# Two layers of attention on one core: a reciprocal, a normalisation and a fold change places in the queues

## The chip, the cores and the metric

One core of one Trainium2 chip runs the whole program. The time is device microseconds of that core, the median of several executions. Engines are named as in the profile: PE is TensorE (matmuls), DVE is VectorE, ACT is ScalarE, POOL is GpSimd, SP is SyncE. Each works through its own queue in order. POOL and SP are used here mostly to issue DMAs.

## The reference

Two layers of the same form, on x of 16 images x 256 channels x 32 x 32, all in float32:

```python
def _L0_conv_ref(x, Wq, bq, Wk, bk, Wv, bv, rel_h, rel_w):
    q = proj(Wq, bq); k = proj(Wk, bk); v = proj(Wv, bv)      # 4 heads of 64, n = 1024
    sim = jnp.einsum('bhdi,bhdj->bhij', q, k)
    rel = (rel_h + rel_w).reshape(heads, d, n)
    qpos = jnp.einsum('hdi,bhdj->bhij', rel, q)
    attn = jax.nn.softmax(sim + qpos, axis=-1)
    out = jnp.einsum('bhdn,bhmn->bhdm', v, attn)
x = x + _L0_conv_ref(_gn(x), ...)       # _gn: 16 groups over the last axis, mean and variance
x = x + _L1_conv_ref(_gn(x), ...)
```

## The kernel before

A **unit** is one image in one layer; there are 32, in an order that leaves several units between the two layers of one image. A unit has four **blocks**: two pairs of heads (`pr`), and for each pair two halves of 512 query columns. The program counts blocks through as n = 4u + b, and "first" to "fourth block" below means b = 0 to 3. All four have their own order, written out by hand: the function `block` serves the second and third block (b = 1, 2), `block_with_q` the first, `block_with_values` the fourth, and `block_without_pieces` the end of the last unit. An engine takes its instructions in just the order in which these functions issue them.

In a block, for each of eight tiles j of 128 keys: DVE writes the positional term as a **seed** into PSUM (`seed`, L442), PE adds the scores (`scores`, L478), ACT takes the exponential into a tile p (L487). Ten p tiles are in rotation. Then PE multiplies p with the values into po (`attend`, L532), and ACT copies po to `od` (`take_out`, L594). The result isn't divided by the softmax's sum until much later, since that sum takes a long way round:

- DVE adds up the p tiles into `acc` (`add_up`, L517 and L519). POOL adds the last one or two of them by accumulating DMAs (`add_last`, L550), each waiting for the one before.
- POOL folds the upper 64 partitions of acc onto the lower (`fold`, L555); SP copies the first 32 of the rest into rows of a `stack` (`stack_up`, L569, two DMAs), and POOL adds the other 32 to the same rows (`fold_again`, L574, two DMAs). Two blocks of one pair of heads share a stack.
- POOL folds the stack in five steps, 64 rows down to 4 (`fold_stack`, L579), spread over the blocks that follow; SP copies the four rows that remain into `den_all` (`spread_sums`, L587, four DMAs).
- DVE takes the reciprocals (`reciprocals`, L629), 16 values on each of 128 partitions. SP writes them to a DRAM tile `rd` (L631) and reads them back spread over all partitions as `rden` (L636, two DMAs).
- DVE multiplies `od` by `rden` (`normalise`, L644), POOL adds the result to x by DMA (`add_by_dma`, L662), and for the second layer SP stores x (`store`, L667).

This takes about a unit: the second block of a unit handles the sums of the first pair of heads of the unit before (`before = blocks[n - 5][:2]`), the fourth block those of its second pair. In both, `reciprocals(*before)` comes early in the block and `normalise(*before)` near its end.

Between these stand pieces of work for coming units: projections, values, and the group norm. In the fourth block the norm's variance for the unit after the next is completed: PE forms a mean, DVE reduces it (`var`, L235), POOL raises it to the power -1/2 (`rstd`, L237) and multiplies once more (`nshift`, L239). In the listing this is `mean_out()`, and in the second block `mean_out()` is the reduction to `neg` (L219), which uses DVE alone.

Before the change, the second block's stack copies and reciprocals stand like this in SP's and DVE's order (L812 to L826):

```python
        if previous and folded:
            stack_up(previous)
        ...
        add_up(blk, 2)
        if before:
            reciprocals(*before)
```

`stack_up(previous)` waits for the fold of the first block, which POOL issues in this same second block.

Of the kernel before, what the change touches and what calls it, by code (L numbers as in the profile page):

```python
# [52 lines left out]
def fast_path(ctx, tc, sh, x, layers, out, W, den_all, good, flag):  # L53
# [457 lines left out]
    def add_up(blk, j):  # L511
        u, pr, half = blk
        if j == 0:
            return
        if j == 1:
            accs[blk] = apool.tile([P, 2, HALF], F32, tag="acc", name=f"acc_{u}_{pr}_{half}")
            nc.vector.tensor_tensor(accs[blk], probs[blk, 0], probs[blk, 1], ALU.add)  # L517
        else:
            nc.vector.tensor_tensor(accs[blk], accs[blk], probs[blk, j], ALU.add)  # L519
# [149 lines left out]
    def finish(u, pr):  # L669
        normalise(u, pr)  # L670
        add_residual(u, pr)
# [85 lines left out]
    def block(n):  # L757
        blk = blocks[n]
        u, b = divmod(n, BPU)
        pr_, half = blk[1:]  # L760

        stacked = blocks[n - 3][:2] if half == 1 and n > 2 else None
        summed = blocks[n - 4][:2] if half == 0 and n > 3 else None
        last_unit = u + 1 == NU
        before = blocks[n - 5][:2] if b == 1 and n > 4 else None
        after = blocks[n + 1] if n + 1 < len(blocks) else None
        previous = blocks[n - 1] if n > 0 else None
        one, two = u + 1 < NU, u + 2 < NU

        pieces = u + 1 < NU or b < 2  # L770
        if u + 1 == NU and b == 1:
            widen(u, 1)
        f0, f1, f2, f3 = ring
        folded = n - 1 < FOLDED
        if not pieces:
            return block_without_pieces(n, half)
        if b == 0 and u > 0:
            return block_with_q(n)
        if b == 3:
            return block_with_values(n)  # L780

        if previous and folded and b == 1:
            add_last(previous, NT - 2)
        elif previous:
            add_up(previous, 6)
            if folded:
                add_last(previous)
            else:
                add_up(previous, 7)
        if b == 2:  # L790
            add_inputs(u + 1, 0)
        for j in range(1 if n > 0 else 2, 4):
            scores(blk, j)
        (first, first_out), (second, second_out) = prepare(u, b)
        first(0)
        norms(u, b, 0)
        if n == 1:
            reduced(2, 1)
            added(2)
        seed(blk, 4, f1)  # L800
        scores(blk, 4)
        add_up(blk, 1)
        norms(u, b, 1)
        second(0)
        if half == 1:
            second_out()
        if stacked:
            fold_stack(*stacked, D)
        if summed:
            fold_stack(*summed, R // 8)  # L810
            spread_sums(*summed)
        if previous and folded:  # L812
            fold(previous)
        if stacked:
            fold_stack(*stacked, R)
        first(1)
        first_out()
        seed(blk, 5, f0)
        scores(blk, 5)
        if previous and folded:  # L820
            stack_up(previous)
        if b == 2 and n > 5:
            store(*blocks[n - 6][:2])
        add_up(blk, 2)
        if before:
            reciprocals(*before)  # L826
        if b == 2:
            add_inputs(u + 1, 1)
        if n == 0:
            reduced(2, 0)  # L830
        if half == 0:
            second(1)
            second_out()
        seed(blk, 6, f1)
        scores(blk, 6)
        if half == 0:
            ring[2:] = f3, f2
        seed(blk, 7, ring[2])
        scores(blk, 7)
        add_up(blk, 3)  # L840
        if b == 2:
            add_inputs(u + 1, 2)
        add_up(blk, 4)

        if after:
            seed(after, 0, f0)
        if n in check:
            next(checks)
        norms(u, b, 2)
        po = psum2(ring[3], f"po_{n}")  # L850
        values_of_p = attend(blk, po)
        values_of_p(0)
        if two and half == 1:
            mean_out = norm_mean(u + 2, filled(f1, f"pm_{n}", 0.0))
        if after:
            scores(after, 0)
        if n == 0:
            mean_out = norm_var(1, filled(f1, f"pm_{n}", EPS / 2))
        if stacked:
            fold_stack(*stacked, R // 2)  # L860
        if previous and folded:
            fold_again(previous)
        if half == 1 and u + 3 < NU and units[u + 3][1] == 0 and u > 0 or n == 3:
            load_x(units[u + 3][0], range(pr_, pr_ + 1) if u > 0 else range(CC))
        add_up(blk, 5)
        if n in (2, 6):
            W.mix(n // 4)
        if before and last_unit:
            finish(*before)
        elif before:  # L870
            normalise(*before)
            add_by_dma(*before)
        if two and half == 1 or n == 0:
            mean_out()
        if stacked:
            fold_stack(*stacked, R // 4)
            if n == len(blocks) - 3:
                fold_stack(*stacked, R // 8)
                spread_sums(*stacked)
        if after:  # L880
            for j in range(1, 4):
                seed(after, j, ring[j % 3])
        norms(u, b, 3)
        values_of_p(1)
        take_out(blk, po)
        pos[n] = po
# [55 lines left out]
    def block_with_values(n):  # L942

        blk = blocks[n]
        u = blk[0]
        r0, r1, r2, r3 = ring
        previous, after, stacked = blocks[n - 1], blocks[n + 1], blocks[n - 3][:2]
        before = blocks[n - 5][:2] if n > 4 else None
        two = u + 2 < NU
        v = Values(u + 1, psum2(r3, f"pw_{u + 1}"))  # L950

        add_last(previous, NT - 2)
        scores(blk, 1)
        add_up(blk, 1)
        one = v.half(1, HI, False), v.half(1, LO, True)
        two_halves = score_half(blk, 2, 0), score_half(blk, 2, 1)
        v.stage("1", (two_halves[0], two_halves[1]), (one[0], one[1]), 0)
        scores(blk, 3)
        v.stage("1", (two_halves[0], two_halves[1]), (one[0], one[1]), 1)
        v.keep(0, 0, 1.0)  # L960
        exponential(blk, 2)
        ab, ab_out = positions(u + 1, 0, psum2(r1, f"pa_{u + 1}_0"))
        ab(0)
        ab_out()
        v.pair("2", 6, 2, 0)
        seed(blk, 4, r0)
        scores(blk, 4)
        v.pair("2", 6, 2, 1)
        v.keep(1, 0, 1.0)
        seed(blk, 5, r2)  # L970
        scores(blk, 5)
        if before:
            reciprocals(*before)
        seed(blk, 6, r1)
        scores(blk, 6)
        v.combine(0, 0, ALU.add)
        fold_stack(*stacked, D)
        fold(previous)
        v.pair("3", 5, 7, 0)
        seed(blk, 7, r0)  # L980
        scores(blk, 7)
        v.pair("3", 5, 7, 1)
        v.keep(1, 1, -1.0)
        fold_stack(*stacked, R)
        stack_up(previous)
        add_up(blk, 2)
        seed(after, 0, r1)
        v.combine(1, 1, ALU.subtract)
        add_up(blk, 3)
        if n in check:  # L990
            next(checks)
        po = psum2(r2, f"po_{n}")
        values_of_p = attend(blk, po)
        values_of_p(0, range(5))
        v.pair("4", 3, 4, 0)
        if two:
            for pr in range(CC):
                bias_x(u, pr)
            mean_out = norm_var(u + 2, filled(r0, f"pm_{n}", EPS / 2))
        values_of_p(0, range(5, NT))  # L1000
        scores(after, 0)
        v.pair("4", 3, 4, 1)
        v.keep(0, 1, -1.0)
        add_up(blk, 4)
        if two:
            mean_out()
        fold_stack(*stacked, R // 2)
        fold_again(previous)
        if u + 3 < NU and units[u + 3][1] == 0:
            load_x(units[u + 3][0], range(1, 2) if u > 0 else range(CC))  # L1010
        ring[:] = r1, r0, r3, r2
        seed(after, 1, r0)
        if before:
            normalise(*before)
        v.combine(1, 0, ALU.add)
        fold_stack(*stacked, R // 4)
        seed(after, 2, r3)
        if before:
            add_by_dma(*before)
        add_up(blk, 5)  # L1020
        seed(after, 3, r1)
        values_of_p(1)
        take_out(blk, po)
        pos[n] = po
# [192 lines left out]
    mean_out = norm_mean(1, pm1)  # L1217
# [322 lines left out]
```

## Time and profile before

| | |
|---|---|
| three runs | 3065.86, 3075.89, 3077.37 us, median 3075.89 |
| profiled execution | 3064.96 us |
| its span, first to last instruction | 3063.2 us |
| mean granted TensorE clock | 0.929 of full speed |
| PE busy | 2593.9 us (85%) |
| DVE busy | 2229.4 us (73%) |
| ACT busy | 2017.4 us (66%) |
| POOL busy | 969.8 us (32%) |
| DMA share of 16 engines | 39.6% issued by POOL, 10.1% by SP |

The span starts with the first instruction and ends with the last; what lies around it is 1.8 us. In each view a group is named by line, engine, operation and the tiles it writes and reads (`od<-od,rden` writes od from od and rden). "idle before <-X" is the time for which the engine stood still ahead of an instruction, and X is what released it. POOL's and SP's rows are the issuing of DMAs; the data land later. The page gives the median time from issue to landing of each kind: 5.1 us for `acc<-p`, 3.5 for `acc<-acc`, 2.1 for `stack<-acc` from SP, 3.1 for `stack<-acc` from POOL, 2.9 for `den_all<-stack`, 2.2 for `rd<-r`, 4.4 for `rden<-rd`, 4.9 for `x<-od`.

### The profile page before, as it was taken

To read this page: it belongs to the slowest core of one execution; us is meant where nothing else is said; L and a number is where in the kernel's file an instruction comes from. 1 tells how busy PE (TensorE), PEld (TensorE's weight loads), DVE (VectorE), ACT (ScalarE), POOL (GpSimd) and SP (SyncE) were. 2 spreads that over 40 slices of the span, in tenths; PEclk is the share of its full clock that TensorE was granted. 3 is DMA by queue.
4 is the path that set the end of the run, shared out by engine and by line. 5 is a ranking of instruction groups with operands and counts; after the bars stand their busy time and mean duration, and the time that the engine had idled before them with its cause. 6 is when DMAs were issued, how large, how long until landed. Compare 5 with 4: busy or idle time off the path is not lost. (4 is left out here: it accounts for less than half of the span.)

```text
span 3063.2 us, 94037 instructions
## 1 busy us (share of the span) xinstructions
PE 2593.9 (85%) x41192; PEld 1453.6 (47%) x41192; DVE 2229.4 (73%) x2184; ACT 2017.4 (66%) x3977; POOL 969.8 (32%) x1029
## 2 busy tenths in 40 slices
PE   8898888978889878898888988789887897878888
PEld 4554444544455444454445544355444554445444
DVE  8786676866768767686676866668766686667878
ACT  7776666766667666675666766667666675667644
POOL 1333233332333323333233332333323333233321
PEclk9999999999999989998999999899999998989999
DMA  3444454555455454555545555454555544544553
GB/s 96 94 88 91 94 98 92 101 112 109 97 105 109 91 100 98 105 95 96 112 95 105 95 98 103 89 117 92 102 115 104 97 83 95 102 88 89 102 106 86
DMA packets 141905, 302.32 MB, mean 99 GB/s; under 512 B 56360, under 2 KB 57896, under 8 KB 141488
## 3 DMA queue, kind: packets, MB, share of 16 engines
q0 software_dynamic: 75744, 210.33, 39.6%
q1 hardware_dynamic: 65744, 85.90, 10.1%
q8 instruction: 326, 5.34, 0.7%
q14 instruction: 91, 0.75, 0.1%
HBM read 51.78 MB, written 17.30 MB: 23 GB/s over the span
## 5 line engine op out<-in xcount | busy, mean ns | idle before, releaser
L487 ACT ACTIVATE p<-ps,shift 128x1024 f32<-128x1024 f32 x993 | 1072.9, 1113 | 845.6 <-PE ps L478 833.1
L478 PE MATMUL ps<-q,k 64*64 64x512 f32 x7944 | 1048.7, 628 | 429.0 <-DVE ps L442 420.9
L442 DVE TENSOR_TENSOR ps<-abt 128x1024 f32<-128x1024 f32 x1018 | 1227.1, 1227 | 190.7 <-ACT p L487 130.0
L532 PE MATMUL po<-p,v 64*64 64x256 f32 x16384 | 943.2, 377 | 15.1 <-ACT q L279 15.1
L532 PEld LDWEIGHTS po<-p,v 64*64 64x64 f32 x16384 | 655.8, 133 | 319.5 <-issue 48.3
L478 PEld LDWEIGHTS ps<-q,k 64*64 64x64 f32 x7944 | 316.0, 139 | 854.5 <-issue 658.9
L519 DVE TENSOR_TENSOR acc<-acc,p 128x1024 f32<-128x1024 f32 x550 | 670.9, 1220 | 2.8
L550 POOL DMA_DIRECT2D acc<-p x217 | 226.0, 1042 | 654.0 <-ACT p L487 168.2
L644 DVE TENSOR_TENSOR od<-od,rden 128x1024 f32<-128x1024 f32 x63 | 77.6, 1231 | 470.4 <-DMA rden<-rd 470.4
L579 POOL DMA_DIRECT2D stack<-stack x310 | 307.0, 990 | 135.9 <-DMA stack<-stack 117.8
L574 POOL DMA_DIRECT2D stack<-acc x248 | 222.0, 1054 | 391.4 <-DMA stack<-acc 384.4
L268 PE MATMUL pq<-xn,Wq 64*64 64x512 f32 x2048 | 246.3, 595 | 0.0
L268 PE MATMUL pk<-xn,Wk 64*64 64x512 f32 x2048 | 243.2, 589 | 0.0
L555 POOL DMA_DIRECT2D acc<-acc x124 | 102.1, 823 | 439.4 <-DMA acc<-p 433.9
L517 DVE TENSOR_TENSOR acc<-p,p 128x1024 f32<-128x1024 f32 x128 | 156.2, 1220 | 92.4 <-ACT p L487 92.4
L248 ACT ACTIVATE xn<-x,nshift,rstd 128x128 f32<-128x128 f32 x496 | 209.6, 494 | 0.0
L237 POOL TENSOR_TENSOR rstd<-var,mhalf 128x16 f32<-128x16 f32 x31 | 122.9, 3964 | 238.3 <-DVE var L235 238.3
L190 ACT ACTIVATE junk<-x,neg 128x128 f32<-128x128 f32 x505 | 198.3, 399 | 0.0
L594 ACT COPY od<-po 128x512 f32<-128x512 f32 x127 | 74.4, 586 | 136.6 <-PE po L532 136.6
L268 PEld LDWEIGHTS pq<-xn,Wq 64*64 64x64 f32 x2048 | 82.2, 138 | 151.2 <-issue 142.4
L190 ACT ACTIVATE junk<-x 128x128 f32<-128x128 f32 x464 | 140.2, 313 | 0.0
L363 PE MATMUL pw<-mixed,t 64*64 64x128 f32 x2976 | 135.6, 271 | 1.8 <-issue 1.8
(96 smaller groups left out, 1921.1 us busy)
## 6 DMA issues: line engine op xcount, KB each, us to landing
acc<-p POOLq DMA_DIRECT2D x217, 512.0 KB, 5.1
rden<-rd SPq DMA_DIRECT2D x126, 256.0 KB, 4.4
acc<-acc POOLq DMA_DIRECT2D x124, 256.0 KB, 3.5
x<-od POOLq DMA_DIRECT2D x61, 512.0 KB, 4.9
x<-in_x_dram SPq DMA_DIRECT2D x32, 512.0 KB, 5.3
stack<-acc SPq DMA_DIRECT2D x248, 64.0 KB, 2.1
stack<-acc POOLq DMA_DIRECT2D x248, 64.0 KB, 3.1
out_dram<-x SPq DMA_DIRECT2D x31, 512.0 KB, 2.9
```

Source lines behind the costliest of these rows:

```text
L190: nc.scalar.activation(junk, grouped(xt[units[u][0]], g), func, accum_out=into[:, g : g + 1], **bias)
L248: nc.scalar.activation(grouped(xns[u], g), grouped(xt[units[u][0]], g), AF.Identity, bias=shift[:, g : g + 1], scale=rstd[:, g : g + 1],)
L268: yield nc.tensor.matmul(pk[c, nh, :], w[l][rs, cc, c0 : c0 + D], xns[u][rs, cc, nh * HALF : (nh + 1) * HALF], start=(t == 0 and cc == 0), ...
L442: nc.vector.tensor_tensor(ps.rearrange("p h (w y) -> p h w y", y=H), ab[:, :, :H].unsqueeze(2).to_broadcast([P, 2, XH, H]), ab[:, :, H + h ...
L478: nc.tensor.matmul(ps[c, h, :], a[hs, j0 : j0 + D], b[hs, columns], start=bool(tag) and i == 0, stop=i == len(terms) - 1, skip_group_check ...
L487: nc.scalar.activation(p, ps, AF.Exp, bias=W.shift)
L517: nc.vector.tensor_tensor(accs[blk], probs[blk, 0], probs[blk, 1], ALU.add)
L519: nc.vector.tensor_tensor(accs[blk], accs[blk], probs[blk, j], ALU.add)
L532: yield nc.tensor.matmul(po[c, a, :QUART], vts[u][rs, pr, j, h * D : (h + 1) * D], p[rs, h, a * QUART : (a + 1) * QUART], start=(t == 0 an ...
L550: nc.gpsimd.dma_start(accs[blk], probs[blk, j], accum_op=ALU.add)
L574: nc.gpsimd.dma_start(at, acc[R:D, h, :], accum_op=ALU.add)
L579: nc.gpsimd.dma_start(stack[:rows_], stack[rows_ : 2 * rows_], accum_op=ALU.add)
```

## The change

Three moves, and no instruction is added or removed. In the second block `reciprocals` goes from behind the second sum to just behind the first sum: on DVE ahead of one seed and one sum, on SP ahead of the two stack copies. In the second block of all units but the last, `normalise` and `add_by_dma` go from ahead of `mean_out()` to behind the three seeds for the block that follows: on DVE behind the reduction to `neg` and three seeds, on POOL behind one fold of the stack. In the fourth block one `fold_stack` and `fold_again` go ahead of `mean_out()`, so on POOL ahead of the power; the sum and the load that are moved with them stay as they were in the queues of DVE and SP.

```diff
@@ def block (second and third block) @@
         scores(blk, 4)
         add_up(blk, 1)
+        if before:
+            reciprocals(*before)
         norms(u, b, 1)
...
         add_up(blk, 2)
-        if before:
-            reciprocals(*before)
         if b == 2:
...
         if before and last_unit:
             finish(*before)
-        elif before:
-            normalise(*before)
-            add_by_dma(*before)
         if two and half == 1 or n == 0:
             mean_out()
         if stacked:
...
             for j in range(1, 4):
                 seed(after, j, ring[j % 3])
+        if before and not last_unit:
+            normalise(*before)
+            add_by_dma(*before)
         norms(u, b, 3)
@@ def block_with_values (fourth block) @@
         v.keep(0, 1, -1.0)
-        add_up(blk, 4)
-        if two:
-            mean_out()
         fold_stack(*stacked, R // 2)
         fold_again(previous)
         if u + 3 < NU and units[u + 3][1] == 0:
             load_x(units[u + 3][0], range(1, 2) if u > 0 else range(CC))
+        add_up(blk, 4)
+        if two:
+            mean_out()
         ring[:] = r1, r0, r3, r2
```

## The prediction

> **What bounds the kernel now.** I read the waits first, then the windows, then the order of time on SyncE (SP), VectorE (DVE) and GpSimd (POOL) through one unit in the middle of the run.
>
> The waits, columns: who waited for whom, us in total, times, longest:
>
> ```profile
> DVE od L644 <- DMA rden<-rd: 470.4, 30, 18.0
> PE ps L478 <- DVE ps L442: 420.9, 34, 16.3
> ACT p L487 <- DMA acc<-p: 8.2, 4, 3.3
> ```
>
> Thirty times, once in each of the 30 units from the second to the last but one, the normalisation (L644) of a second block holds DVE for 470.4/30 = 15.7 us until the reciprocals have come back spread out as rden. The seeds stand behind it on DVE, so TensorE (PE) is starved: 420.9 us is 90% of its idle time, since 3063.2 - 2593.9 = 469.3 us. The windows (PE, PEld, DVE, ACT, POOL busy, then clock, DMA share, GB/s) show a saturated PE before and nothing during:
>
> ```profile
> 1560.00:1574.00 14.00, 14.00 (x244) 7.35 (x240) 11.59 (x12) 12.74 (x30) 4.08 (x5) 1.00 0.42 77
> 1574.00:1588.00 14.00, 2.08 (x40) 1.18 (x32) 0.00 (x0) 2.33 (x6) 4.30 (x6) 0.74 0.58 111
> 1588.00:1600.00 12.00, 9.13 (x72) 3.25 (x76) 11.84 (x12) 5.21 (x9) 3.86 (x5) 0.73 0.49 92
> ```
>
> Why rden is late is told by SP in order of time, columns start, length, instruction:
>
> ```profile
> 1556.73 2.89 SPq L587 DMA_DIRECT2D den_all<-stack  x4
> 1560.19 20.66 SPq L569 DMA_DIRECT2D stack<-acc  x4
> 1580.90 0.58 SPq L631 DMA_DIRECT2D rd<-r  x1
> 1583.14 1.31 SPq L636 DMA_DIRECT2D rden<-rd  x2
> ```
>
> and by DVE:
>
> ```profile
> 1524.51 0.25 DVE L629 RECIPROCAL r<-den_all 128x16 f32<-128x16 f32 x1
> 1535.17 1.24 DVE L644 TENSOR_TENSOR od<-od,rden 128x1024 f32<-128x1024 f32 x1
> ...
> 1564.44 0.25 DVE L629 RECIPROCAL r<-den_all 128x16 f32<-128x16 f32 x1
> 1588.13 1.23 DVE L644 TENSOR_TENSOR od<-od,rden 128x1024 f32<-128x1024 f32 x1 [16.50 <-DMA rden<-rd]
> ```
>
> The reciprocal is done at 1564.7, but its copy rd is issued at 1580.90. In SP's queue it stands behind the two copies into the stack (the last two of the x4), which wait for POOL's fold of the first block (L555, issued 1576.25, landing 3.5 later). In the fourth block the same pair, not queued so, needs no wait with 1535.17 - 1524.51 = 10.7 us between.
>
> **Part 1, the reciprocal up.** Removed: nothing; 31 reciprocals of 0.25 us move ahead of one seed and one sum on DVE (1.14 us each by their starts, 2.3 together), so from 1564.44 to 1562.2. SP issues rd and two rden ahead of two stack copies: 0.6 + 1.3 = 1.9 us, against copies that wait until 1579.8 anyway; the wait covers them, and uncovered they would cost the fold chain 1.9 us a unit. rd goes at 1562.5, lands 2.2 later; rden is issued 1564.7 to 1566.0 and lands 4.4 later, 1570.4. New on DVE: the reciprocal may wait for den_all. Its four copies are issued by 1559.6 and land in 2.9: 1562.5. Behind it wait a seed and the sums, so scores and PE. By this it costs 0.3 us a unit, nothing if POOL runs the 3 us earlier that part 3 can give, and 2 if POOL runs 2 late; a gain of its own it can't have, since nothing waits for r but the chain to rden. I take 0.
>
> **Part 2, normalisation down.** It leaves its place ahead of neg and three seeds (1493.96 to 1497.6) and stands behind them: on an unstalled DVE at 1571.6 + 3.7 = 1575.3, against rden at 1570.4. Room 4.9 us; the 470.4 us are gone, and the seeds come 1.1 us earlier. The sixth sum and the inputs' sum behind it are no later than before. On POOL the add into x (L662) goes behind a fold of the stack.
>
> What remains of a unit: from the first stalled normalisation, 154.06, to the last, 2933.71, are 29 units of 95.85 us. Less PE's idle time, 420.9/30 = 14.0, and less the half clock after it. The first 24 score matmuls after the stall took 4.33 us (1590.87 to 1595.20), while 8 took 0.86 (1596.92 to 1597.78): 4.33 - 2.58 = 1.75. Left: 80.1. PE's busy time says 2593.9/32 - 1.75 = 79.3; the last unit, which doesn't stall, goes from normalisation to normalisation in 3012.16 - 2933.71 = 78.45, with less work on ACT and POOL. So PE by itself would need 79 to 80.
>
> **Part 3, the fourth block's fold ahead of the power.** POOL, today:
>
> ```profile
> 1524.72 0.80 POOL L555 DMA_DIRECT2D acc<-acc  x1 [3.81 <-DMA acc<-p]
> 1525.39 0.94 POOL L579 DMA_DIRECT2D stack<-stack  x1
> 1534.08 3.96 POOL L237 TENSOR_TENSOR rstd<-var,mhalf 128x16 f32<-128x16 f32 x1 [7.75 <-DVE var L235]
> 1538.12 0.97 POOL L239 TENSOR_TENSOR nshift<-neg,rstd 128x16 f32<-128x16 f32 x1
> 1539.04 0.84 POOL L579 DMA_DIRECT2D stack<-stack  x1
> 1539.63 2.00 POOL L574 DMA_DIRECT2D stack<-acc  x2
> 1542.64 0.82 POOL L579 DMA_DIRECT2D stack<-stack  x1 [1.01 <-DMA stack<-stack]
> 1543.17 1.22 POOL L662 DMA_DIRECT2D x<-od  x1
> 1543.74 1.54 POOL L550 DMA_DIRECT2D acc<-p  x1
> 1551.18 0.86 POOL L550 DMA_DIRECT2D acc<-p  x1 [5.90 <-ACT p L487]
> ```
>
> Moved: one stack fold and two adds of acc. If POOL is on time they fill the 7.75 us wait for var, and what follows the power starts 3 us sooner. If POOL is late, they are dear: the adds wait for the stack copies, some 6.4 us after the fold, and today the power's 5.0 us lie inside that wait; afterwards they come on top. The price is 0 to 5 us a unit on POOL.
>
> So POOL's own chain has to be added up, each link from the starts of this unit and its neighbours, as if nothing else held it. First block: two adds of p in series, 7.5 with the add into x just ahead; fold 5.2 later; its adds 6.4 later; 1.2 to issue: 20.3. Second: 6.0 + 5.3 + 6.1 + 2.3 (adds, stack fold, x): 19.7. Third: one add of p to the fold 4.9, which becomes 7.1 since the add into x now stands straight ahead of it as in the first block; 6.5; 1.2: 14.8. Fourth: 5.3 + 5.9 + 6.4 + 1.2, power 5.0, stack fold and x 1.1: 24.9. Sum 79.7 us a unit. Today that hides in 95.85. Afterwards it is as long as PE's 79 to 80, and two loops of equal length that wait for each other (POOL for sums and p; ACT for a p buffer that POOL's add frees, a wait that the trace shows four times already; DVE for den_all) run somewhat longer than either. I take 81 us, with 79.3 below and 84 above (twelve landings 0.35 us longer, as DMA share rises from 0.50 to 0.50 x 95.85/81 = 0.60).
>
> **Sum.** 30 units x (95.85 - 81.0) = 445. 3063.2 - 445 = 2618 us span. The profiled execution took 3064.96, the runs 3065.86 to 3077.37, median 3075.89, some 0.3% more: 2625 for the median.
>
> A rule of the Trainium skill that speaks against the change: "DMA: Bandwidth & Descriptors", Latency and other measured facts, gives HBM access 0.2 us on average and 2 at high load. The trace shows rd and rden, which pass through DRAM, landing in 2.2 and 4.4 us at a DMA share of 0.58. As an estimate by that page, 1.8 us more on each of the two would turn the room of 4.9 into 1.3 and still leave no wait.
>
> **Rivals.** B: POOL never shows, PE alone sets 79.3 us: 3063 - 30 x 16.55 = 2567. For it: POOL waits for compute in every block today. Against it: the 79.7 above.
> C: each of POOL's twelve landings lengthens by 0.35 to 0.85 us: 84 to 90 us a unit, 2708 to 2888. For it: part 3 takes the power out of its cover. Against it: today's stretch without PE has a DMA share of 0.58 and its landings are in the sum already.
> D: the wait moves instead of going. den_all is late, the reciprocal holds DVE for half of the old stall: 3063 - 30 x 7 = 2853. Against it: the first wait would start at 0.3 us, not at 8.
> E, the other side: the late POOL chain itself passes the old unit. It decides from 95.85 - 79.7 = 16.1 us more, which is 1.35 us on each of twelve landings; at 1.6 us the unit is 98.9 and the time 3063 + 30 x 3 = 3155. For it: all of POOL's links are in series. Against it: no landing in this trace is so long in the middle, 5.1 us for adds of p and 3.5 for folds.
>
> **Numbers.** Forecast 0.62, with 2580 to 2705 as its own range (80 to 84 us a unit); B 0.14; C 0.14; D 0.05; E 0.03; no measurable difference (within 0.5%, about what a measurement of this kernel can tell) 0.02, if the copies wait for something that I didn't see. Range 2565 to 2720: it takes in B and the near end of C, and leaves out the rest of C, D, E and no difference, together 0.2. Faster by over 0.5%: 0.95, same 0.02, slower 0.03.
>
> **What would show it.** Right: L644 no longer waits for rden, PE's wait for the seeds falls from 421 to below 60 us, the granted clock rises from 0.929 to above 0.98, rd starts within 1 us of its reciprocal, POOL's wait for var falls from 7.75 us towards 0 or 3, and new short waits appear at ACT p L487 for acc<-p or at L629. Wrong: a wait of several us at L629, or at L644 still; or units above 84 us with POOL waiting only for its own landings.

## The result, and the profile after

| | before | after |
|---|---|---|
| median | 3076.63 us (4 runs) | 2755.28 us (2753.04 to 2760.36, 4 runs) |
| ratio, 95% interval | 1 | 0.8961, 0.8933 to 0.8989 |
| profiled execution, its span | 3063.2 us | 2758.6 us |
| granted clock over the span | 0.929 | 0.972 |

The change is worth 10.4%, and it stays 35 us above the top of the forecast range. The waits of after (who waited for whom, us in total, times, longest) show the old wait gone and others in its place:

```profile
POOL acc L555 <- DMA acc<-p: 508.7, 124, 6.8
...
ACT xn L248 <- POOL nshift L239: 132.8, 29, 8.3
...
PE ps L478 <- DVE ps L442: 106.6, 62, 6.4
...
ACT p L487 <- DMA acc<-p: 51.4, 33, 4.4
...
POOL rstd L237 <- DVE var L235: 28.2, 1, 28.2
...
DVE r L629 <- DMA den_all<-stack: 18.1, 13, 5.2
...
DVE od L644 <- DMA rden<-rd: 11.5, 9, 2.2
```

L644's wait has fallen from 470.4 to 11.5 us, PE's wait for seeds from 420.9 to 106.6. New is ACT's wait for `nshift`, once in nearly every unit. And POOL waits for var only once, in the first unit (28.2 us). In the profile of before it did so in every unit, 7.0 us each in the mean without the first:

```profile
POOL rstd L237 <- DVE var L235: 238.3, 31, 28.2
```

Now POOL comes to the power when var has long been there.

SP and DVE in order of time (start, length, instruction), one second block:

```profile
1584.26 1.17 SPq L569 DMA_DIRECT2D stack<-acc  x2
1585.70 0.36 SPq L631 DMA_DIRECT2D rd<-r  x1
1587.17 1.11 SPq L636 DMA_DIRECT2D rden<-rd  x2
1605.31 1.13 SPq L569 DMA_DIRECT2D stack<-acc  x2
```

```profile
1585.41 0.25 DVE L629 RECIPROCAL r<-den_all 128x16 f32<-128x16 f32 x1 [1.67 <-DMA den_all<-stack]
...
1598.65 1.22 DVE L644 TENSOR_TENSOR od<-od,rden 128x1024 f32<-128x1024 f32 x1
```

Now rd is issued at once, 0.3 us after the start of its reciprocal, and the normalisation, 13.2 us after the reciprocal, finds rden there. That is the change as meant. What POOL makes of the fourth block is seen in its order of time, with DVE's var ahead of it:

```profile
1548.99 0.18 DVE L235 TENSOR_REDUCE var<-pm 128x16 f32<-128x32 f32 x1
```

```profile
1551.64 0.81 POOL L555 DMA_DIRECT2D acc<-acc  x1 [5.30 <-DMA acc<-p]
1552.16 1.09 POOL L579 DMA_DIRECT2D stack<-stack  x1
1555.87 0.77 POOL L579 DMA_DIRECT2D stack<-stack  x1 [2.62 <-DMA stack<-stack]
1558.66 1.71 POOL L574 DMA_DIRECT2D stack<-acc  x2 [2.02 <-issue]
1559.79 4.57 POOL L237 TENSOR_TENSOR rstd<-var,mhalf 128x16 f32<-128x16 f32 x1
1564.43 0.22 POOL L239 TENSOR_TENSOR nshift<-neg,rstd 128x16 f32<-128x16 f32 x1
...
1588.06 1.47 POOL L550 DMA_DIRECT2D acc<-p  x1
1595.66 0.86 POOL L550 DMA_DIRECT2D acc<-p  x1 [6.13 <-DMA acc<-p]
```

DVE had var ready at 1549.2; the power starts at 1559.79, behind the adds that wait for the stack copies. In the median of the 28 units described below, it starts 10.2 us after var is ready (0.1 us in before). Who pays is told by ACT, DVE and PE in order of time:

```profile
1564.69 0.49 ACT L248 ACTIVATE xn<-x,nshift,rstd 128x128 f32<-128x128 f32 x1 [5.46 <-POOL nshift L239]
...
1566.21 1.23 DVE L442 TENSOR_TENSOR ps<-abt 128x1024 f32<-128x1024 f32 x1 [4.62 <-ACT p L487]
...
1567.50 1.74 PE L478 MATMUL ps<-q,k 64*64 64x512 f32 x8 [3.49 <-DVE ps L442]
```

ACT stands 5.46 us at the apply of the norm; the exponentials behind it are late, so a PSUM tile comes free late for DVE's seed, and PE stands 3.49 us. From power to power POOL takes 85.3 us in the mean of the 28 units in which it issues the same instructions in the same order (95.9 before), and its long waits there are for landings, of its own DMAs and of SP's stack copies. (The waits of an add of p at L550 that the listing puts down to ACT are, nearly all, second adds, 5 to 8 us after the first. They too wait for that one's landing: they start 0.5 to 0.8 us after it.) POOL goes round on its own, and compute follows.

### The profile page after: what moved, and what is told of

Its sections match the earlier page's. It is cut to its first block, busy times and chain, and to the rows that moved or that the text cites. A ratio compares the mean times of both kernels' runs of the same rounds, so it can differ in the third digit from the quotient of the medians.

```text
span 2758.6 us, 94006 instructions
## 1 busy us (share of the span) xinstructions
PE 2599.2 (94%) x41192; PEld 1424.4 (52%) x41192; DVE 2233.9 (81%) x2184; ACT 2012.0 (73%) x3977; POOL 937.2 (34%) x1029
## 5 line engine op out<-in xcount | busy, mean ns | idle before, releaser
L478 PE MATMUL ps<-q,k 64*64 64x512 f32 x7944 | 1003.6, 600 | 111.5 <-DVE ps L442 106.6
L532 PE MATMUL po<-p,v 64*64 64x256 f32 x16384 | 990.1, 390 | 26.5 <-ACT q L279 25.3
L478 PEld LDWEIGHTS ps<-q,k 64*64 64x64 f32 x7944 | 289.1, 133 | 521.8 <-DVE ps L442 259.8
L550 POOL DMA_DIRECT2D acc<-p x217 | 269.6, 1242 | 543.8 <-DMA acc<-p 219.2
L574 POOL DMA_DIRECT2D stack<-acc x248 | 214.2, 985 | 454.7 <-DMA stack<-acc 422.2
L268 PEld LDWEIGHTS pk<-xn,Wk 64*64 64x64 f32 x2048 | 74.2, 134 | 125.3 <-issue 123.3
L363 PEld LDWEIGHTS pw<-mixed,t 64*64 64x64 f32 x2976 | 114.3, 133 | 38.3 <-DVE v L405 20.4
L363 PE MATMUL pw<-Wv,xn 64*64 64x128 f32 x1984 | 133.6, 273 | 0.3 <-issue 0.3
```

Of the source, the lines that this page charges most:

```text
L268: yield nc.tensor.matmul(pk[c, nh, :], w[l][rs, cc, c0 : c0 + D], xns[u][rs, cc, nh * HALF : (nh + 1) * HALF], start=(t == 0 and cc == 0), ...
L363: yield nc.tensor.matmul(self.pw[c, a, part * P : (part + 1) * P], x[rs, j0 : j0 + D], w[rs, :], start=first and not whole and part == 0, ...
L478: nc.tensor.matmul(ps[c, h, :], a[hs, j0 : j0 + D], b[hs, columns], start=bool(tag) and i == 0, stop=i == len(terms) - 1, skip_group_check ...
L532: yield nc.tensor.matmul(po[c, a, :QUART], vts[u][rs, pr, j, h * D : (h + 1) * D], p[rs, h, a * QUART : (a + 1) * QUART], start=(t == 0 an ...
L550: nc.gpsimd.dma_start(accs[blk], probs[blk, j], accum_op=ALU.add)
L574: nc.gpsimd.dma_start(at, acc[R:D, h, :], accum_op=ALU.add)
```

## The experiments

All ratios are to the kernel before, run on the same chip, with their 95% intervals. The experiments ran on three chips, so kernels are compared by their ratios. Three theories are set against each other in what was expected. In the loop theory POOL's own chain of DMAs sets the unit. In the second, only the place of the power counts, through ACT's wait for nshift. In the contention theory DMAs take longer to land as the unit shrinks. Where a link of POOL's chain is given below, it is the time from one start to the next, the median over the same 28 units of one profiled execution.

**Part 3 undone.**

```diff
@@ block_with_values, against after @@
+        add_up(blk, 4)
+        if two:
+            mean_out()
         fold_stack(*stacked, R // 2)
         fold_again(previous)
...
-        add_up(blk, 4)
-        if two:
-            mean_out()
```

> Parts 1 and 2 alone: the fourth block's fold stays behind the power. Loop theory: after the change POOL's own chain, 85.4 us from power to power, sets the unit, and every us taken off it is worth 30 us. Here the power's 5 us go back under the 6 to 7 us wait for the stack copies, so the loop is 80 to 81 us: 2755 - 30 x 4.5 = 2620, within 2590 to 2650, and ACT's wait for nshift (133 us in all) is gone. Contention theory: the landings grow as the unit shrinks (adds of p from 5.1 to 6.0 us), so the loop gives back more than half: 2690 or more. Theory that only the power's place counts: 2755 - 133 = 2622.

Measured: 2688.31 us, 0.8774 (0.8754 to 0.8795). Part 3 costs some 57 us on top of the others, 2.0 us a unit by POOL's loop (83.3 for 85.3), half of what the loop theory expected; "2690 or more", of the contention theory, is nearly met. Without part 3 the fourth block is 2.8 us shorter in the mean, but the first is 0.9 longer. The waits:

```profile
ACT p L487 <- DMA acc<-p: 131.2, 71, 5.7
...
PE ps L478 <- DVE ps L442: 81.2, 77, 3.2
...
DVE r L629 <- DMA den_all<-stack: 40.9, 26, 3.2
...
ACT xn L248 <- POOL nshift L239: 9.2, 7, 2.8
```

ACT's wait for nshift is nearly gone, yet compute waits nearly as long as in after, now for p buffers and den_all: the four waits together, ACT's for nshift and for p buffers and DVE's for den_all and for rden (L644, 10.7 here), come to 192 us, for 214 in after. So nshift was only the place where the late POOL was felt. The theory that only the power's place counts (2622) falls.

**Part 3 alone.** The same edit as part 3 on the kernel before.

> Part 3 alone on the kernel before. Loop theory: POOL is on time there and waits 7.8 us for var, the fold and the adds fit into that wait, nothing changes: 3070 to 3080. Theory that only the power's place counts: the power comes after the adds whatever the rest does, nshift is late and ACT waits: 3100 or more.

Measured: 3016.3 us, 0.985 (0.9829 to 0.9871): faster by 1.5%, which neither theory had. The wait of L644 is 427.0 us here instead of 470.4. With the fold and the adds done before the power, POOL needs 2.5 us from nshift to the next add of p instead of 4.6 (medians of its starts). The first block's fold, for which SP's stack copies wait, comes 1.8 us earlier after var in the mean, and with it rd behind them; L644's wait is 1.4 us a unit shorter. My expectation left out that the old stall hung on POOL's chain.

**One add of p from POOL to DVE.**

```diff
@@ block, against after @@
         if previous and folded and b == 1:
-            add_last(previous, NT - 2)
+            add_up(previous, 6)
+            add_last(previous)
```

> After, but in the second block one of POOL's two adds of p goes to DVE (one sum of 1.2 us more a unit on an engine that is 81% busy). Loop theory: the link of 8.0 us between the two adds goes from POOL's loop, 77 to 78 us are left, PE's 79 to 80 us set the unit: 2590 to 2620, no wait of ACT for nshift. Theory that only the power's place counts: 2755, within 15. Contention theory: one 512 KB transfer less, landings back by a part: 2680 to 2720.

Measured: 2635.43 us, 0.8606 (0.8583 to 0.8629). One link less is worth 4.0% by the ratios, although DVE has 33 us more to do. It is above the expected 2590 to 2620, as POOL's loop still sets 81.4 us; ACT's wait for nshift is down to 40.1 us with the power in the same place, which again speaks against the place.

**The add into x later.**

```diff
@@ block, against after @@
         if previous and folded:
             fold(previous)
+        if b == 2 and n > 5:
+            add_by_dma(*blocks[n - 6][:2])
...
             normalise(*before)
-            add_by_dma(*before)
```

> After, but the second block's add into x is issued in the third block behind the fold, where POOL waits for the stack copies, instead of straight ahead of the add of p. Loop theory: the link from that add to the fold goes from 8.1 to about 6 us, 2 us a unit off the loop: 2755 - 60 = 2695, within 2680 to 2715. Theory that only the power's place counts: no change, 2755. Contention theory: the transfer collides with the stack copies instead, 2740 to 2770.

Measured: 2759.56 us, 0.9016 (0.8996 to 0.9037): no gain, against the loop theory's 2695, and within the contention theory's 2740 to 2770. By POOL's starts the link from the third block's add to its fold did shrink, from 7.9 to 5.7 us, but the next, fold to its adds, grew from 6.9 to 8.5 with the transfer now in it, and the fourth block's fold to its adds from 6.4 to 7.6. The unit stayed at 85.1, and ACT's copy of po got a wait of its own for the late add (`od` buffers, 85.3 us, 27 times). This transfer, moved within the loop, didn't leave it.

**Part 1 alone, and part 2 alone.** Each is its own lines of the change on the kernel before.

> Part 1 alone on the kernel before. Loop theory: rden is on its way from about 1.5 us after the reciprocal and lands some 10 us after it, about when the normalisation in its old place comes up, so the wait of 15.7 us shrinks to 0 to 2 and POOL's loop (83.3 us without part 3) sets the unit here too: ratio to before 0.877 to 0.888. Theory that the place of the normalisation is what hides the wait: more than half of the gain is missing, ratio 0.94 or more.

Measured: 2666.3 us, 0.8704 (0.8675 to 0.8733). Part 1 alone is better than all three, and a little better than expected. L644 waits 45.0 us in all, 1.5 a unit.

> Part 2 alone on the kernel before. rd still stands behind the stack copies on SP, rden still lands some 16 us too late for the old place, and the new one is 3.6 us later: the wait falls from 15.7 to about 12 us a unit, ratio 0.96 to 0.97. If the place of the normalisation is what hides the wait, ratio below 0.93.

Measured: 2997.82 us, 0.9799 (0.9783 to 0.9816). L644 still waits 349.8 us, 11.7 a unit, as expected; but the gain is one to two points smaller than expected. PE's wait for the seeds falls less than DVE's wait, from 420.9 to 350.1 us, and the span is shorter by just about that (2993.3 for 3063.2). Why PE gains less than DVE was not followed up.

**Parts 1 and 2 with the add into x ahead of the stack fold.** This asks why part 2 on top of part 1 loses (0.8774 against 0.8704).

```diff
@@ block, against parts 1 and 2 @@
+        late = before and not last_unit
         if stacked:
-            fold_stack(*stacked, R // 4)
+            if not late:
+                fold_stack(*stacked, R // 4)
...
             normalise(*before)
             add_by_dma(*before)
+            fold_stack(*stacked, R // 4)
```

> Parts 1 and 2 without part 3, but on POOL the second block's add into x stays ahead of the stack fold, as in part 1 alone, while the normalisation stays behind the seeds. If the order on POOL is what makes parts 1 and 2 slower than part 1 alone (the add into x straight ahead of the third block's add of p): ratio 0.870. If the later normalisation itself is: 0.877.

Measured: 2654.15 us, 0.8656 (0.8631 to 0.8681). The order on POOL it is: the normalisation is as late as in parts 1 and 2, and one DMA ahead of another is worth 1.2%. POOL's unit is 0.9 us shorter, and 0.5 of that is the link from the third block's add of p to its fold (7.9 to 7.4 us). That this kernel is also better than part 1 alone, by the later normalisation, is not shown: the two intervals touch, and POOL's unit is 82.4 us in both.

**A second read beside rden.**

```diff
@@ reciprocals (twice=True in the second block alone), against after @@
+        if twice:
+            spare = dpool.tile([P, 2 * HALF], F32, tag="spare", name=f"spare_{u}")
+            for h, hs in enumerate(QUARTERS):
+                nc.sync.dma_start(
+                    spare[hs, : count * HALF],
+                    rd[h : h + 1].to_broadcast([D, count * HALF]),
+                )
```

> After, and in the second block the 512 KB read that makes rden is followed by a second one of the same size from the same rd into a DRAM tile that nothing reads; the result is as before. Theory that company on the DMA engines lengthens POOL's links: the link between the two adds of p, 6.0 us before the change and 8.0 after it, where rden is now read in its midst, grows by another 1 to 2.5 us, and since POOL's loop sets the unit, the ratio rises from 0.896 to 0.91 to 0.925. Rival, the link is longer because of POOL's own lateness or its queue and not by the company: link 8.0, ratio 0.896 within 0.005.

Measured: 2772.18 us, 0.9041 (0.9004 to 0.9078). The link between the adds is 8.4 us, 0.5 more, and the ratio is 0.8 points up: the direction of the company theory, but half of the least that it expected. What is firm is that the link is 6.2 and 5.8 us in the two kernels without part 1 (parts 3 and 2 alone), 6.0 before, and 7.4 to 8.0 in all five with part 1 that have this link and no second read (part 1 alone, parts 1 and 2 in both orders, after, the later add into x). That rden's bytes alone make the 2 us is not shown. The second read is also no copy of the first: it goes from DRAM to DRAM and leaves SBUF alone, while rden and the adds of p are written into SBUF. Whether it is the writes into SBUF that get in each other's way was not tried.

**One add on DVE, without part 3; then two adds.** The second adds this to `block_with_q`:

```diff
-        add_last(previous, NT - 2)
+        add_up(previous, 6)
+        add_last(previous)
```

> Parts 1 and 2 and the second block's add of p on DVE, without part 3. Loop theory: POOL's loop, 80.8 us with part 3, loses 2 more and is shorter than PE's 79 to 80 us, so PE sets the unit: 2600 to 2625 (ratio 0.850 to 0.858). Contention theory (landings stretch to whatever the unit is): no gain over the same kernel with part 3, ratio 0.861.

Measured: 2584.57 us, 0.8446 (0.8431 to 0.8461), better than expected.

> As the kernel with one add of p on DVE and without part 3, and the first block's add goes to DVE as well, so another link of about 8 us leaves POOL's loop (some 71 us). Loop theory: the loop no longer sets anything, POOL waits for compute again (for var, for sums), and the time is PE's floor: 2590 to 2620 and no more than 15 us under the kernel with one such add. If DVE, at 86% with one, becomes the bound: 2630 or more.

Measured: 2566.64 us, 0.8383 (0.8369 to 0.8397), the best of all, 6.4% under after by the ratios. It is below the expected 2590 to 2620, and 18 us under one add, where 15 was the most expected: PE's floor is lower than I took it to be there. The span, 2566.6 us, is the 2567 that rival B of the prediction gives for PE alone. The waits of the kernel with two adds on DVE have the line that after had lost:

```profile
POOL rstd L237 <- DVE var L235: 206.3, 31, 28.2
PE ps L478 <- DVE ps L442: 1.9, 2, 1.3
```

and the chain that ended last, which in after was followed back through DMAs for 3% of the span and then lost, is PE's from end to end:

```profile
PE 90%; ACT 3%; issue 3%; DVE 3%; DMA 0%; SPq 0%; ACTq 0%; DVEq 0%
```

POOL waits for compute again, PE is busy for 98% of the span, and the unit is 79.1 us.

**Part 1 alone with two adds on DVE.**

> Part 1 alone with two adds of p on DVE. With POOL's loop off the path the later normalisation can only help: with it in the old place DVE waits 1 to 2 us a unit for rden, PE has some scores in hand, so 0 to 30 us more than the kernel with parts 1 and 2 and the two sums: ratio 0.838 to 0.848. If the place of the normalisation is worth nothing even then: 0.838.

Measured: 2570.38 us, 0.8397 (0.8383 to 0.8411). With POOL's loop out of the way part 2 is worth 0.1%, no more than the intervals allow for nothing, and the old place of the normalisation waits 2.8 us for rden in the whole run.

| kernel | ratio | POOL, power to power |
|---|---|---|
| parts 1, 2, 3 (after) | 0.8961 | 85.3 us |
| parts 1, 2 | 0.8774 | 83.3 |
| part 1 | 0.8704 | 82.4 |
| parts 1, 2, add into x first | 0.8656 | 82.4 |
| after, one add on DVE | 0.8606 | 81.4 |
| parts 1, 2, one add on DVE | 0.8446 | 79.7 |
| parts 1, 2, two adds on DVE | 0.8383 | 79.1 |

The last column is the mean over the 28 units of one profiled execution that issue in the same order, so a few tenths in it mean little.

## Why the prediction was wrong

**Right: the cause of the old stall and its end.** rd stood behind the stack copies; put ahead of them it takes nearly the whole wait away. Part 1 alone shows it: 470.4 us at L644 become 45.0. The prediction gave the end of the wait to part 2 (room 4.9 us at the later place); part 1 does nearly all of it.

**Right: PE's own 79 to 80 us a unit.** The two kernels with two adds on DVE, in which POOL waits for var in every unit, run at 79.1 and 79.2.

**Right in kind: POOL's loop becomes the bound, and part 3 is dear when POOL is late.** Both were in the text, the second at 0 to 5 us a unit. It was 57 us, 2 a unit. The last sign of being wrong that the prediction names, units above 84 us with POOL waiting only for its own landings, is what came, but for SP's copies that it waits for as well.

**Wrong: the term "POOL's own chain, 79.7 us a unit".** It measures 85.3, where the prediction took 81 for the whole unit, and 30 x (85.3 - 81.0) = 129 of the 140 us between the predicted span of 2618 and 2758.6 come from there. By its parts (predicted, then after, over the 28 units, as a sum of the links' medians and of their means):

| | predicted | after, medians | after, means |
|---|---|---|---|
| first block | 20.3 | 20.0 | 20.7 |
| second block | 19.7 | 22.0 | 22.6 |
| third block | 14.8 | 16.0 | 16.2 |
| fourth block with the power | 24.9 | 25.4 | 25.8 |
| sum | 79.7 | 83.4 | 85.3 |

Two errors stand in the second and third block, 2.3 and 1.2 us. In the second, the link between two adds of p was taken from a trace in which rden was read 17.7 us after the first of them (1583.14 and 1565.40). Part 1 puts the read of 512 KB (issued 1587.17 to 1588.28) straight onto the add that starts at 1588.06, and the link went from 6.0 to 8.0. That part 1 brings this is shown, that it is by the read's company is argued. In the third, the price for the add into x straight ahead was taken as 2.2 us and was 3.0, and the wait for the stack copies behind it grew by 0.4. The rest, 85.3 - 83.4, is no link at all: I added up middling values of one unit and its neighbours, and a chain in series takes its mean, tails included. The link between the first block's two adds is 7.5 us in the median and 7.9 in the mean.

**Wrong by its chances: rival C.** It had the time (2708 to 2888) and got 0.14, but its mechanism held only in part, so its time was right partly by luck. C had all twelve landings longer. The profile's median for adds of p went from 5.1 to 6.0 us, while folds (3.5) and SP's stack copies (2.1) did not change. And the adds of p did not all lengthen (medians from issue to landing, before, then after): the first block's two 7.0 and 4.8, then 6.9 and 4.6; the second's 5.5 and 4.9, then 7.4 and 4.8; the third's one 4.6, then 7.6; the fourth's two 4.9 and 5.6, then 5.6 and 5.9. The long ones are those to which the change moved rden's read and the add into x. What spoke against C, "its landings are in the sum already", was true of the places where nothing new came close, and false of these two.

**Missed: who waits for nshift.** Part 3's price was given for POOL's queue only. In the trace of before ACT asks for xn at 1543.62 and nshift is done at 1539.09, 4.5 us of room; a power that starts 10 us after var instead of at once uses that up. It was not what made the time, as the runs without part 3 and with one add on DVE show, but it is the largest new wait of compute on POOL in the profile of after.

**The rule on DRAM.** The Trainium skill, "DMA: Bandwidth & Descriptors", Latency and other measured facts, has 2 us for HBM under high load against 0.2. Here rd went from 2.2 to 2.5 us and rden from 4.4 to 4.8 when the DMA share rose from 0.50 to 0.56; the estimate of 1.8 us more on each was far too high, and L644 waited 11.5 us in the whole run. The transfers that did lengthen, POOL's adds, lie in SBUF on both sides.

## What to carry to other kernels

When a stall goes, the engine that was idle behind it sets the new time: add up each in-order queue that issues dependent DMAs, link by link, as a loop of its own, with means and not middling values, and with the transfers that the change itself brings together. A move that hides work in an engine's wait is worth something only while that wait is there; moves that were worth 1.5% and 2% alone (parts 3 and 2) cost 2% and 0.8% on top of part 1, so parts of one change are to be measured alone and together. If compute waits for a late queue, taking away the wait that the profile lists first only lets the next one show; a link has to leave the loop, here an add that moved to an engine with room.

## What the runs showed of the hardware that was not expected

An accumulating DMA of 512 KB within SBUF lands 2 to 3 us later with another of its size issued straight ahead of it: the third block's add of p in 7.6 us instead of 4.6, and its link to the fold takes 7.9 us instead of 4.9, and 5.7 with the other one moved away. The order of two DMAs on POOL that differ 32 times in size (add into x and a stack fold) is worth 1.2% of the whole time. The number of bytes alone isn't the price: 512 KB more of company in the same link cost 0.5 us where the first 512 KB came with 2, though the second went to DRAM and the first into SBUF.

PE's waits cost it twice, by the wait and by a slower clock behind it. Apart from the start and the end of the run, the kernels in which PE never waited for more than 3.2 us had a granted clock of 0.994 and more. It was 0.988 with the later add into x, where PE waited up to 5.0 us behind ACT's copies, and 0.972 in after, with waits for seeds of up to 6.4. PE was busy 2599.2 us there for the work that took 2560.5 without part 3. Since POOL's loop sets the unit in after, it is not shown that these 39 us cost any time. The Trainium skill, "TensorE: Matmul & The Clock Gate", Part 1, puts the idle window after which the clock is halved at about 3.4 us. Here a shorter wait was enough: in after PE waits 2.76 us until 1653.78, and the granted clock is 0.50 from 1653.70 to 1659.90 and 1.00 from 1646.00 to 1651.00. Most of the half-clock stretches of after follow waits of 2.7 to 3.4 us.
